# A state space layer put into a written order on four engines, with GpSimd two groups ahead and one behind, and a window attention with four score banks

## The chip, the cores and the metric

The kernel runs on one core of one Trainium2 chip. A core has five engines that run side by side, each with its own queue of instructions and ordered among each other by semaphores only: TensorE (PE, matrix products, with a separate row PEld for the loading of weights), VectorE (DVE), ScalarE (ACT), GpSimd (POOL) and SyncE (SP, which here issues every DMA). SBUF is the working memory, PSUM [...] takes the results of PE. The metric is the device time of the whole program in microseconds (us), as the median of several runs.

## The reference

Four images of 384 channels and 64 x 64 pixels go through two residual layers, all in float32. Each first normalizes its input over 32 groups of 12 channels (group norm).

```
x = x + state_space(gn(x))
x = x + window_attention(gn(x))

state_space, on L = 4096 tokens in row order:
  xn = layer norm over the 384 channels
  xb, z = split(xn @ in_proj)                     # 768 channels each
  xc = silu(causal conv of 4 taps over tokens (xb))
  dt, B, C = split(xc @ x_proj)                   # 24, 16 and 16 columns
  dt = softplus(dt @ dt_w + dt_b)
  for each token t, channel c, state n of 16:
      h[c,n] = exp(dt[t,c] * A[c,n]) * h[c,n] + dt[t,c] * xc[t,c] * B[t,n]
      y[t,c] = sum over n of h[c,n] * C[t,n]
  out = ((y + xc * D) * silu(z)) @ out_proj

window_attention: 12 heads of 32 channels; each pixel attends to the 7 x 7
  pixels around it (edge padded) with a relative bias; then a projection
```

## The kernel before, in words

The program takes one image after another: statistics of the input, `layer0` (state space), `layer1` (attention).

`layer0` holds channels in partitions (six blocks `d` of 128 channels) and tokens along the row, and works in 16 chunks of T = 256 tokens. In a chunk it runs over the six blocks and over four groups `g` of four states: 24 groups, each one call of `scan`. A group needs `db`, the product of dt, x and B for four states, 128 x 1024, which `driven` computes on GpSimd (L439, with `dtx` for a new block in L434). `scan` then works in two halves of two states: ScalarE computes da = exp(dt A) into one of the two PSUM banks of `ps_a` (L457), VectorE runs the recurrence along the tokens (L460), first into PSUM (`hp`), then into SBUF (`hs`); the last column is kept as the state for the next chunk (L466, L470). The product with C is VectorE's for `hp` (L467, into `hv`) and GpSimd's for `hs` (L471). PE transposes both against the identity and adds them up in `y` (L478). After four groups `turned` copies y on ScalarE (L488), turns it back on PE and adds xc D (L491, L496); `gated` multiplies with silu(z) (L504, VectorE). After six blocks `out_proj` runs (L516, L522).

Beside the scans of chunk i the preparation of chunk i+1 goes on. It is a Python generator (`prepared`, with `normed` called from it through `behind`), and `scan` takes one step of it with `next(ahead)` twice per group. `normed` is the group norm (L281, VectorE), the mean over channels by a product with ones (L287), subtraction, square, mean of squares, root by Ln and Exp, multiplication. `prepared` is the input projection (L310), the convolution as four products with diagonal matrices (L317), biases on ScalarE, six Silu in one block with a table load before and after, the product for dt, B and C (L331) with a trip of B and C through memory to spread them over partitions, and three softplus.

The order on the engines isn't that of the Python code: a planner orders each queue by its own estimates of costs. The order of the code only gives priorities, and the table-bound functions of ScalarE are kept in order by hand (`in_order`).

`layer1` works in eight stripes of eight rows, each with four blocks of 8 x 16 pixels, each with three steps `m` of four heads. A step is `scores` (four products of K = 32 rows into banks of `ps_l`, L727, a reduction on VectorE that adds the bias and finds the maximum, L733, an Exp on ScalarE), then for the step two back `attended` (L775), and for the one before `weighted`, the transposes of the weights (L752, L763) with their copies (L757, L767). At a block's end `block_end` turns the sums (L786 to L795), at a stripe's end `stripe_end` projects (L809, L814). Between, `projected` makes q, k and v of the next stripe (L632, L665, L695), one bank `mm` at a time; `window` loads the block of v that a block of pixels sees.

In the bank count of PSUM layer0 uses 2 + 1 + 2 + 3 = 8 (`ps_a`, `ps_h`, `ps_y`, `ps`), layer1 3 + 2 + 1 + 2 = 8 (`ps_l`, `ps_t`, `ps_v`, `ps`).

Of the kernel before, what the change touches and what calls it, by code (L numbers as in the profile page):

```python
# [8 lines left out]
F32 = mybir.dt.float32  # L9
AF = mybir.ActivationFunctionType  # L10
ALU = mybir.AluOpType
# [37 lines left out]
def two_layers(  # L49
# [22 lines left out]
    NB = x.shape[0]  # L72

# [180 lines left out]
    def layer0(b, x1, gm, st1):  # L254
        with ExitStack() as es:
            ps_a = es.enter_context(tc.tile_pool(name=f"ps_a{b}", bufs=2, space=PSUM))
# [6 lines left out]
            gm = gm(ps)  # L263

# [6 lines left out]
            def normed(i, h):  # L271
# [8 lines left out]
                for j in range(NJ):  # L280
                    nc.vector.tensor_scalar(  # L281
                        xn[:, j, :], src[:, j, :], gm[:, j, 0:1], gm[:, j, 1:2],
                        ALU.subtract, ALU.mult,
                    )
                mv = bank()
# [7 lines left out]
                )  # L293
                act(sq, xn, AF.Square)
                for j in range(NJ):
                    nc.tensor.matmul(
                        mv[:, 1, :], ones_c, sq[:, j, :], start=(j == 0), stop=(j == NJ - 1)
                    )
# [79 lines left out]
            def prepared(i, h):  # L378
# [31 lines left out]
                yield  # L410
                late = h["late"]()
                next(late, None)
                for t in h["xc"] + h["sz"]:
                    act(t, t, AF.Silu)
                load_exp_ln()
                yield
# [27 lines left out]
            def scan(d, g, h, db, y, ahead):  # L444
# [7 lines left out]
                hs = w2.tile([P, 2, T], F32, tag="hs", name="hs", bufs=3)  # L452
                for half, to in ((0, hp), (1, hs)):
# [11 lines left out]
                    if half == 0:  # L465
                        nc.vector.tensor_copy(state[:, d, n : n + 2], hp[:, :, T - 1])  # L466
                        nc.vector.tensor_tensor(hv, hp, ct[:, 0:2, :], ALU.mult)  # L467
                        next(ahead, None)
                    else:
                        nc.gpsimd.tensor_copy(state[:, d, n : n + 2], hs[:, :, T - 1])  # L470
                        nc.gpsimd.tensor_tensor(hs, hs, ct[:, 2:4, :], ALU.mult)  # L471

                for t in (hv, hs):
# [9 lines left out]
                next(ahead, None)  # L483
# [68 lines left out]
            db, late, ahead, y = driven(*work[0], steps[0]), None, iter(()), None  # L552
            done = iter(())
            for at, (i, d, g) in enumerate(work):
                if d == 0 and g == 0:
# [4 lines left out]
                    ahead = next_step()  # L560
                if g == 0:
                    y = ps_y.tile([P, 2, P], F32, tag="y", name="y")
                if (d, g) == (ND - 1, NS // NG - 1):
                    all_of(ahead)
                now = db
                if at + 1 < len(work):
                    nxt = work[at + 1]
                    db = driven(*nxt, steps[nxt[0]])
                scan(d, g, steps[i], now, y, ahead)
                next(done, None)  # L570
                if g == 3 and late is not None:
                    gated(*late)
                    if late[1] == ND - 1:
                        done = out_proj(late[0], late[2])
                if g == 1 and late is not None:
                    late = turned(*late)
                if g == NS // NG - 1:
                    late = (i, d, steps[i], y)
            late = turned(*late)
# [5 lines left out]
    def layer1(b, x1, gm):  # L585
        scale = HD**-0.5
        with ExitStack() as es:
            ps_l = es.enter_context(tc.tile_pool(name=f"ps_l{b}", bufs=3, space=PSUM))
            ps_t = es.enter_context(tc.tile_pool(name=f"ps_t{b}", bufs=2, space=PSUM))
            ps_v = es.enter_context(tc.tile_pool(name=f"ps_v{b}", bufs=1, space=PSUM))  # L590
            ps = es.enter_context(tc.tile_pool(name=f"ps1_{b}", bufs=2, space=PSUM))
# [209 lines left out]
            def stripe_end(s, aT):  # L801
                for m in range(NJ):
# [16 lines left out]
                    )  # L819

            pending, turned = None, None

            def attend():
# [4 lines left out]
                if m == NJ - 1:  # L828
                    block_end(bl, blk, aT)
                    if bl == NBLK - 1:  # L830
                        stripe_end(s, aT)
# [5 lines left out]
            for s in range(NXT):  # L837
# [5 lines left out]
                for bl in range(NBLK):  # L843
# [4 lines left out]
                    for m in range(NJ):  # L848
# [8 lines left out]
                        next(ahead, None)  # L857
# [7 lines left out]
            attend()  # L865

# [60 lines left out]
```

## Time and profile before

| | |
|---|---|
| time, median of 3 | 10455.0 us (10454.19 to 10461.72) |
| PE busy | 8126.5 us, 78% of the span |
| DVE busy | 7762.4 us, 74% |
| POOL busy | 6045.2 us, 58% |
| ACT busy | 5652.8 us, 54% |
| PEld busy | 5786.0 us, 55% |
| mean granted PE clock | 0.866 |
| scans of the first image | 178 to 1948 us |
| attention of the first image, first to last score | 2012 us to about 2670 us |

The share over the whole span averages two stages with different limits, so it is of little use by itself; the profile cuts the span in 40 slices and gives the busy tenths of each. A row of the groups reads: line, engine, operation, output from input with shapes and how often; then the busy time in all and the mean duration in nanoseconds of one; then the idle time of that engine just before these instructions and what ended it. A row of the waits reads: the engine and what it wanted to do, the work that released it, then the total in us, the number of times and the longest. A row of the timeline reads: start and length in us, engine, line, operation, shapes; in brackets the idle time before it.

### The profile page before, as it was taken

What the parts mean: (1) busy time and instruction counts of PE and PEld (TensorE: products, weight loads), DVE (VectorE), ACT (ScalarE), POOL (GpSimd) and SP (SyncE); (2) the same over time, 40 slices, a digit from 0 to 9 for tenths busy, and PEclk for the clock granted to TensorE, in tenths of its full rate; (3) what the DMA queues carried; (4) which work ended last, traced back from release to release, by engine and by line L of the source; (5) the groups of instructions that cost most, each with busy time, mean ns of one, the idle gap of its engine ahead of it and who ended that gap; (6) DMA issues with size and microseconds to landing.
All of it is one profiled execution on the core that took longest, in us unless ns stands there. A gap on an engine that the chain in (4) does not pass through costs nothing. (4 is left out here: it accounts for less than half of the span.)

```text
span 10459.5 us, 141089 instructions
## 1 busy us (share of the span) xinstructions
PE 8126.5 (78%) x46266; PEld 5786.0 (55%) x46266; DVE 7762.4 (74%) x15536; ACT 5652.8 (54%) x13502; POOL 6045.2 (58%) x5279
## 2 busy tenths in 40 slices
PE   4777777799777777779967777777996777777899
PEld 4565565455556556545556556554555556555455
DVE  4888888655588888855568888885556888888555
ACT  3666666344466666634446666653444666665344
POOL 3888888400388888830048888882005888888100
PEclk9888888799788888889978888888998888888899
DMA  2111111122111111112211111112212111111221
GB/s 79 55 42 41 53 42 40 59 75 65 67 46 42 51 43 42 50 58 79 58 68 42 43 51 42 45 46 69 70 56 69 39 55 42 41 53 38 71 71 54
DMA packets 300180, 563.69 MB, mean 54 GB/s; under 512 B 61197, under 2 KB 183325, under 8 KB 298805
## 3 DMA queue, kind: packets, MB, share of 16 engines
q1 hardware_dynamic: 299444, 554.67, 16.3%
q8 instruction: 366, 6.00, 0.2%
q14 instruction: 370, 3.02, 0.1%
HBM read 452.01 MB, written 84.73 MB: 51 GB/s over the span
## 5 line engine op out<-in xcount | busy, mean ns | idle before, releaser
L93 ACT ACTIVATE da<-dt,nega 128x256 f32<-128x256 f32 x6144 | 2902.2, 478 | 1563.9 <-DVE hs L460 851.0
L439 POOL TENSOR_TENSOR db<-dtx,B 128x1024 f32<-128x1024 f32 x1536 | 3619.7, 2357 | 0.0
L478 PE MATMUL y<-ident,hs 128*128 128x128 f32 x6144 | 1205.8, 329 | 1788.1 <-POOL hs L471 1785.9
L460 DVE TENSOR_TENSOR_SCAN hs<-da,state,db 128x256 f32<-128x256 f32 x3072 | 2217.6, 733 | 352.9 <-ACT da L93 333.9
L460 DVE TENSOR_TENSOR_SCAN hp<-da,state,db 128x256 f32<-128x256 f32 x3072 | 2290.1, 745 | 239.5 <-ACT da L93 101.5
L478 PEld LDWEIGHTS y<-ident,hs 128*128 128x128 f32 x6144 | 814.6, 165 | 2205.4 <-POOL hs L471 2180.5
L471 POOL TENSOR_TENSOR hs<-hs,C 128x512 f32<-128x512 f32 x1536 | 1949.5, 1269 | 5.4
L786 POOL COPY rb<-rsum 128x384 f32<-128x384 f32 x128 | 69.3, 541 | 2379.1 <-DVE rsum L784 2291.9
L310 PE MATMUL mm_ps<-xn,w_in 128*128 128x256 f32 x4608 | 1218.8, 404 | 7.7 <-DVE xn L303 7.7
L478 PE MATMUL y<-ident,hv 128*128 128x128 f32 x6144 | 1174.3, 325 | 46.4 <-DVE hv L467 46.0
L93 ACT ACTIVATE sg<-sg,mx 128x308 f32<-128x308 f32 x1536 | 830.9, 542 | 544.2 <-DVE mx L733 539.9
L478 PEld LDWEIGHTS y<-ident,hv 128*128 128x128 f32 x6144 | 926.2, 169 | 263.9 <-DVE hv L467 89.1
L467 DVE TENSOR_TENSOR hv<-hp,C 128x512 f32<-128x512 f32 x1536 | 1043.0, 679 | 0.0
L310 PEld LDWEIGHTS mm_ps<-xn,w_in 128*128 128x128 f32 x4608 | 898.6, 207 | 122.5 <-DVE xn L303 10.3
L470 POOL COPY state<-hs 128x2 f32<-128x2 f32 x1536 | 292.2, 190 | 1163.7 <-DVE hs L460 1048.5
L733 DVE CUSTOM_DVE_ANT_0 sg<-lg_ps,bias 128x308 f32<-128x308 f32 x1536 | 672.9, 475 | 322.2 <-PE lg_ps L727 269.6
L727 PE MATMUL lg_ps<-k,q 32*128 32x308 f32 x3072 | 695.2, 477 | 138.5 <-DVE mx L733 129.7
L317 PE MATMUL mm_ps<-xb,dcv 128*128 128x256 f32 x3072 | 748.9, 380 | 0.0
L767 ACT COPY tb<-pt_ps 88x512 f32<-88x512 f32 x384 | 223.2, 581 | 898.4 <-PE pt_ps L763 884.3
L757 DVE COPY ta<-pt_ps 110x512 f32<-110x512 f32 x768 | 494.0, 681 | 201.8 <-PE pt_ps L752 173.4
L317 PEld LDWEIGHTS mm_ps<-xb,dcv 128*128 128x128 f32 x3072 | 556.5, 191 | 63.3
L727 PEld LDWEIGHTS lg_ps<-k,q 32*128 32x128 f32 x3072 | 267.1, 185 | 521.9 <-DVE mx L733 290.1
(136 smaller groups left out, 11076.0 us busy)
## 6 DMA issues: line engine op xcount, KB each, us to landing
B<-bcrows SPq DMA_DIRECT2D x256, 512.0 KB
C<-bcrows SPq DMA_DIRECT2D x256, 512.0 KB
vw<-vd SPq DMA_DIRECT2D x1792, 33.0 KB
xr<-x SPq DMA_DIRECT2D x28, 1056.0 KB
vd<-v SPq DMA_DIRECT2D x280, 96.0 KB
xi<-in_x_dram SPq DMA_DIRECT2D x64, 384.0 KB
x<-in_x_dram SPq DMA_DIRECT2D x32, 768.0 KB
x<-xo SPq DMA_DIRECT2D x64, 384.0 KB
```

The costliest lines, as they stand in the source:

```text
L93: ins = nc.scalar.activation(o, i, func, **kw)
L310: nc.tensor.matmul(pb[:, k, :], w_in[:, j, m * P : (m + 1) * P], xn[:, j, :], start=(j == 0), stop=(j == NJ - 1),)
L317: nc.tensor.matmul(pb[:, k, :], dcv[:, d, c, :], xb[:, d, c : c + T], start=(c == 0), stop=(c == KC - 1),)
L439: nc.gpsimd.tensor_tensor(db, h["dtx"].unsqueeze(1).broadcast_to([P, NG, T]), h["bc"][g][0], ALU.mult)
L460: nc.vector.tensor_tensor_scan(to[:, k, :], da[:, k, :], db[:, 2 * half + k, :], state[:, d, n : n + 1], ALU.mult, ALU.add,)
L467: nc.vector.tensor_tensor(hv, hp, ct[:, 0:2, :], ALU.mult)
L470: nc.gpsimd.tensor_copy(state[:, d, n : n + 2], hs[:, :, T - 1])
L471: nc.gpsimd.tensor_tensor(hs, hs, ct[:, 2:4, :], ALU.mult)
L478: nc.tensor.matmul(y[:, half, :], t[:, k, half * P : (half + 1) * P], ident, is_transpose=True, start=(first and half == 0), stop=(last an ...
L727: nc.tensor.matmul(lg[:, :NK], blk["q"][pr, m, bl, :, :].rearrange("p r c -> p (r c)"), blk["k"][pr, m, :, bl * CB : bl * CB + CW], start= ...
L733: nc.vector.tensor_tensor_reduce(sg[:, hh, :], lg[:, :NK], bias[:, 4 * m + hh, :], -1.0, BIG, ALU.add, ALU.min, mx[:, hh : hh + 1],)
L757: nc.vector.tensor_copy(t[: KN[0], :, :].rearrange("p a q -> p (a q)"), pt[: KN[0], :])
```

## The change

In `layer0` the four compute engines leave the planner: inside `tc.manual_schedule(engines=in_step)` their queues have the order of the Python code (the DMA queue stays planned). The code is rewritten for that. GpSimd's `db` is made two groups ahead of the scans instead of one; its product of `hs` with C (now `with_c`) comes one group after the scans, and the sums on PE one group (`hv`) and two groups (`hs`) after. `hs` gets a fourth buffer. The group norm moves from VectorE to ScalarE, as scale and bias of an Identity, with `gb` = -mean x rstd. The chain of the layer norm gets more `yield`, so that each engine's part stands half a group after the one that feeds it. `turned` comes one group later and the gated product stays in the group after it.

In `layer1` the scores get four PSUM banks and the general pool `mm` one instead of two. So that the output projection needs only one bank at a time, `stripe_end` becomes a generator: one of its three parts in each of the following steps, in the place of a step of `projected`. The planner still orders this layer.

```
+    E = mybir.EngineType
+    in_step = {E.DVE, E.Activation, E.PE, E.Pool}
...
     def layer0(b, x1, gm, st1):
+            es.enter_context(tc.manual_schedule(engines=in_step))
...
+            gb = w1.tile([P, NJ, 1], F32, tag="gb", name=f"gb_{b}")
+            nc.vector.scalar_tensor_tensor(
+                gb, gm[:, :, 0:1], -1.0, gm[:, :, 1:2], ALU.mult, ALU.mult
+            )
...
                 for j in range(NJ):
-                    nc.vector.tensor_scalar(
-                        xn[:, j, :], src[:, j, :], gm[:, j, 0:1], gm[:, j, 1:2],
-                        ALU.subtract, ALU.mult,
-                    )
+                    act(
+                        xn[:, j, :], src[:, j, :], AF.Identity, scale=gm[:, j, 1:2],
+                        bias=gb[:, j, :],
+                    )
+                yield
...
+                yield
                 act(sq, xn, AF.Square)
+                yield
...
-                hs = w2.tile([P, 2, T], F32, tag="hs", name="hs", bufs=3)
+                hs = w2.tile([P, 2, T], F32, tag="hs", name="hs", bufs=4)
...
-                    else:
-                        nc.gpsimd.tensor_copy(state[:, d, n : n + 2], hs[:, :, T - 1])
-                        nc.gpsimd.tensor_tensor(hs, hs, ct[:, 2:4, :], ALU.mult)
-
-                for t in (hv, hs):
+                next(ahead, None)
+
+                def with_c():
+                    nc.gpsimd.tensor_copy(state[:, d, n : n + 2], hs[:, :, T - 1])
+                    nc.gpsimd.tensor_tensor(hs, hs, ct[:, 2:4, :], ALU.mult)
+
+                def summed(t):
...
+                return with_c, lambda: summed(hv), lambda: summed(hs)
...
+            AHEAD = 2
+            dbs = [driven(*w, steps[w[0]]) for w in work[:AHEAD]]
...
+                if at + AHEAD < len(work):
+                    if work[at + AHEAD][1:] == (0, 0):
+                        all_of(ahead)
...
+                if before:
+                    before[0][0]()
+                if at + AHEAD < len(work):
+                    nxt = work[at + AHEAD]
+                    dbs.append(driven(*nxt, steps[nxt[0]]))
+                if before:
+                    before[0][1]()
+                if len(before) > 1:
+                    before.pop()[2]()
                 next(done, None)
...
+                before.insert(0, scan(d, g, steps[i], dbs.pop(0), ys[d], ahead))
+                if g == 2 and late:
+                    late[0] = turned(*late[0])
+                if g == 3 and late:
+                    gated(*late[0])
...
     def layer1(b, x1, gm):
-            ps_l = es.enter_context(tc.tile_pool(name=f"ps_l{b}", bufs=3, space=PSUM))
+            ps_l = es.enter_context(tc.tile_pool(name=f"ps_l{b}", bufs=4, space=PSUM))
-            ps = es.enter_context(tc.tile_pool(name=f"ps1_{b}", bufs=2, space=PSUM))
+            ps = es.enter_context(tc.tile_pool(name=f"ps1_{b}", bufs=1, space=PSUM))
...
+                    yield True
...
-                        stripe_end(s, aT)
+                        ends.append(stripe_end(s, aT))
...
-                        next(ahead, None)
+                        if ends and next(ends[0], None) is None:
+                            ends.pop()
+                        elif not ends:
+                            next(ahead, None)
```

## The prediction

> **What bounds the kernel now.** I read the busy tenths first, because the program has two kinds of stages, four of each (one pair per image): the state space layer and the attention.
>
> ```profile
> PE   4777777799777777779967777777996777777899
> ...
> DVE  4888888655588888855568888885556888888555
> ...
> POOL 3888888400388888830048888882005888888100
> PEclk9888888799788888889978888888998888888899
> ```
>
> In the state space slices VectorE (DVE) and GpSimd (POOL) stand at 8 and TensorE (PE) at 7; in the attention slices PE stands at 9 and GpSimd at 0. First and last scan of each image lie 1769 us apart (178 to 1948 us in the first), so four layers take 7076 us; the rest is about 690 us of attention per image and the gaps around it.
>
> The groups of instructions by line name the work of the state space layer.
>
> ```profile
> L439 POOL TENSOR_TENSOR db<-dtx,B 128x1024 f32<-128x1024 f32 x1536 | 3619.7, 2357 | 0.0
> L460 DVE TENSOR_TENSOR_SCAN hs<-da,state,db 128x256 f32<-128x256 f32 x3072 | 2217.6, 733 | 352.9 <-ACT da L93 333.9 <-POOL db L439 5.5 <-PE y L478 5.4
> L471 POOL TENSOR_TENSOR hs<-hs,C 128x512 f32<-128x512 f32 x1536 | 1949.5, 1269 | 5.4
> L281 DVE TENSOR_SCALAR xn<-xi,gm_a 128x256 f32<-128x256 f32 x192 | 280.8, 1517 | 105.2 <-PE mm_ps L310 105.1
> ```
>
> 1536 is the number of "groups" (4 images x 16 chunks x 6 channel blocks x 4 state groups), so a group takes 1769/384 = 4.61 us and a chunk of 24 groups 110.6 us. The durations overlap at their ends, so I take pitches from the timeline, here GpSimd alone:
>
> ```profile
> 511.71 2.37 POOL L439 TENSOR_TENSOR db<-dtx,B 128x1024 f32<-128x1024 f32 x1
> 514.02 1.27 POOL L471 TENSOR_TENSOR hs<-hs,C 128x512 f32<-128x512 f32 x1
> 515.23 0.20 POOL L470 COPY state<-hs 128x2 f32<-128x2 f32 x1
> 515.37 2.37 POOL L439 TENSOR_TENSOR db<-dtx,B 128x1024 f32<-128x1024 f32 x1
> ```
>
> One group costs GpSimd 515.37 - 511.71 = 3.66 us, and every fourth one 0.73 us more (dtx, L434): 24 x 3.66 + 6 x 0.73 = 92.2 us per chunk. On VectorE the same timeline gives 3.39 us from scan to scan of undisturbed groups (511.15 to 514.54): 81.4 us, plus what it does once per chunk. So neither engine alone explains 110.6 us: they lose by waiting for each other. The waits say so.
>
> ```profile
> POOL state L470 <- DVE hs L460: 1048.5, 585, 7.5
> ACT da L93 <- DVE hs L460: 851.0, 803, 3.1
> DVE hs L460 <- ACT da L93: 333.9, 219, 2.8
> DVE yg L504 <- PE mm_ps L496: 293.7, 92, 4.8
> ```
>
> Taking the starts of the db products and their differences by place in the chunk shows where. The first 15 groups take 62.7 us (most are 3.66 or 4.4 us, one is 6.6 us at the wait for L496), the last nine 48.0 us, of which one group takes 10.1 us. That one is this, on VectorE:
>
> ```profile
> 460.78 5.28 DVE L281 TENSOR_SCALAR xn<-xi,gm_a 128x256 f32<-128x256 f32 x3
> 465.98 0.41 DVE L504 TENSOR_TENSOR yg<-mm_ps,sz 128x256 f32<-128x256 f32 x1
> 468.12 0.95 DVE L291 TENSOR_TENSOR xn<-xn,mm_ps 128x768 f32<-128x768 f32 x1 [1.74 <-PE mm_ps L287]
> ```
>
> **What the Trainium skill says.** "SBUF — State Buffer", section "SBUF: two separate sides": VectorE in a 2-port mode and GpSimd take one pair of ports under an exclusive lock, and the loser waits for the whole instruction. L281 agrees: 399 ns at best, 3820 ns at worst, mean 1517 ns, beside db products of 2357 ns. "TensorE: Matmul & The Clock Gate", Part 1: the PE clock is granted by activity. The trace agrees: 1.00 in attention, 0.71 in the sparse end of a chunk (697 to 734 us). Part 3 of the same page: matmuls on different 32-row strips of the array run side by side. It agrees too: six score passes take 0.80 us and two take 0.79 us. The specification table there calls the queues of the other engines strict first-in first-out, which matters for the written order.
>
> **The change part by part, state space layer.** Its four engines leave the planner and run in the order of the Python code.
>
> Group norm (L281) goes to ScalarE. VectorE loses 5.3 us per chunk; ScalarE gains 3 x 0.47 (an Identity of that shape, the xb row) = 1.4 us. ScalarE is about 61% busy (63 us of 100), so the sum fits, but where it stands matters: the three lie just ahead of the six Silu and two table loads, which in the trace run from 458.90 to 465.45 us with a 0.8 us piece of other work between, thus 5.8 us. No exponentials pass them. The timeline has 0.99 us for a pair of exponentials; ScalarE can be at most two pairs (the two da banks) ahead of the scans. From the end of one pair ScalarE needs 1.4 + 0.4 (ys copy) + 1.0 + 5.8 + 1.0 = 9.6 us to the second pair after it; VectorE has about 4.4 us of scans for that time. It stalls about 5.2 us per chunk. So of the 6.7 us that the 10.1 us group is too long, most stays: the L281 that went was lying beside this ScalarE block.
>
> The chain of the normalization (mean, subtract, square, mean, root, multiply) gets a yield between each engine, so the 1.74 us wait of L291 falls away.
>
> GpSimd: db two groups ahead of the scans, hs times C one group behind. No operation is added; the product no longer waits for the scan just ended, and the scans have two db in store. PE sums hv one group and hs two groups late, so the 1785.9 us that PE waits for hs should go; they cost little directly, but ScalarE's biases and the gated product (3.3 us, the 6.6 us group) queue behind PE. The gated product now comes a step after its transposes. New constraint: PE stands in line behind hs of two groups ago, and ScalarE's bias work behind PE; GpSimd may lag by perhaps half a group (2 us) and not by two.
>
> Sum for a chunk. First 15 groups: GpSimd 15 x 3.66 + 4 x 0.73 = 57.8 us; VectorE 15 x 3.39 + 3 gated x 0.4 + residual 1.1 + statistics 1.1 = 54.3. PE waits 13.2 of 63 us there, so needs 49.8. GpSimd bounds, less about 1.5 us of lag it may make up later: 56.3. Last nine: VectorE 30.5 + softplus 9 x 0.67 = 6.0 + L291 and L303 1.9 + gated 1.2 = 39.6, plus the 5.2 stall = 44.8; GpSimd 34.4; ScalarE 9 x 1.9 + softplus 10.8 + the rest some 10 = 38. Together 101.1 us against 110.6: 9.5 us x 64 chunks = 610 us. Bounds: perfect decoupling gives VectorE's 92.9 (24 x 3.39 + 11.5) plus part of the stall, 96.5 us (gain 900); if every ScalarE wait costs as before, 108 us (gain 170).
>
> **Attention.** It stays with the planner. With three score banks the fourth head waits for VectorE's first reduction:
>
> ```profile
> 10057.41 0.80 PE L727 MATMUL lg_ps<-k,q 32*128 32x308 f32 x6
> 10058.77 0.79 PE L727 MATMUL lg_ps<-k,q 32*128 32x308 f32 x2 [0.56 <-DVE mx L733]
> 10059.49 0.64 PE L775 MATMUL pv_ps<-ta,vw 110*32 110x128 f32 x16
> ```
>
> From the first score to pv is 2.08 us; one step earlier, where six passes were followed by pv at once, it is 0.73. Four banks give about 1.35 us less; VectorE's copies of ta then start later relative to PE, so I count 1.1. In the built order nine of a stripe's twelve steps have four scores in a row: 10 us of the 85.5 us of a stripe, seven stripes per image (the last has no projections), 70 us. Against it stands the single mm bank. In a stripe's end the built order puts three q projections nearly in a row, because the output projection, now spread over steps, has taken three or four steps of the next stripe's projections; each waits for a 0.75 us eviction: about 2 us. The last v rows reach memory later, two steps before their window is loaded, and that window's fourteen transfers take 6 us to issue: 0 to 4 us, I take 1.5. In all 3.5 x 7 = 25. The first projection of an image (42 us, fifteen banks in a row) can't overlap eviction with matmuls any more: some 5 us more beyond what the half clock hides. Net 70 - 25 - 5 = 40 us per image, 160 us in all; between 0 and 300.
>
> Forecast: 10455 - 610 - 160 = 9685 us.
>
> **Rivals.** (A) The forecast, 9685. (B) Both engines run near their own sums: 96.5 us a chunk and the full attention gain, 10455 - 900 - 300 = 9255. For it: the 3.66 us runs are exact, so nothing but waits stands between. Against it: the Silu block and five groups of softplus, where ScalarE is nearly full. (C) The written order only moves the waits: PE's cold clock at the start of a chunk delays the biases, these delay exponentials in a strict queue, 108 us a chunk, and the single bank eats the attention's gain: 10455 - 170 - 50 = 10235. For it: the 0.71 clock, and that each group already needs all four engines. (D) Convoys: each queue blocked by its oldest wait, a group at 5.1 us, or 122.4 us a chunk: 64 x 11.8 = 755 us lost, 160 gained: 11050. For it: a planner filled gaps that no order of mine can see. Against it: in the built order every cross-engine pair stands at least half a group apart.
>
> **How the numbers follow.** A 0.60, B 0.15, C 0.18, D 0.07. The likeliest gives 9685. A with its own spread and C make up 0.78; the range from 9320 (between A and B) to 10100 (most of C) leaves out about 0.2. Faster by over 0.2%: A, B and C but for a little, 0.92; within 0.2%: 0.01; slower: 0.07.
>
> **What would show it.** Right: db products 4.2 us apart on average; L281's successor on ScalarE at about 0.47 us each; the waits of PE for hs nearly gone; GpSimd at 9 tenths in the state space slices; one gap of about 5 us per chunk left at the Silu block; score passes in eights with pv 0.8 us after. Wrong: VectorE waiting for da at every group (ScalarE in line behind PE), GpSimd waiting for hs scans as before, PE waiting for q's eviction or for the window at each stripe's end, or a stripe still at 85 us.

## The result, and the profile after

The changed kernel takes 10500.5 us (median, 10500.0 to 10504.6) against 10457.9 us before: a ratio of 1.0042, 95% interval [1.0024, 1.0059]. It is slightly slower, where 9685 us had been forecast. Line numbers from here on are those of the changed kernel (db L453, scans L474, hv L481, state copy and product on GpSimd L486 and L487, sums L495, softplus' products L370 and corrections L384 to L386, all of ScalarE's functions L96).

First the busy tenths of the changed kernel, to be laid beside those of before.

```profile
PE   4677777699777777769967777777996777777799
...
DVE  3888888655588888865568888886556888888655
...
POOL 3788878500388878850048878884004877888300
PEclk9788878799878877879988877887998877887899
```

VectorE still stands at 8 and GpSimd at 7 to 8, not at 9, and the clock granted to TensorE is a tenth lower in many of these slices (mean 0.847, before 0.866). In the first image the first and last scan lie 1821 us apart (185.5 to 2006.9 us) instead of 1769, so four state space layers lost some 208 us; the program as a whole lost 43, so the rest gained about 165.

The page's groups confirm that GpSimd's two products did not become dearer (mean ns behind the bar, 2357 and 1269 before); the scans stay at 0.73 to 0.75 us:

```profile
L453 POOL TENSOR_TENSOR db<-dtx,B 128x1024 f32<-128x1024 f32 x1536 | 3613.2, 2353 | 30.1
...
L487 POOL TENSOR_TENSOR hs<-hs,C 128x512 f32<-128x512 f32 x1536 | 1944.8, 1266 | 123.2 <-POOL state L486 0.8
```

The successor of L281 on ScalarE takes 100.5 us in all. What changed is who waits for whom (total us, times, longest):

```profile
POOL state L486 <- DVE hs L474: 1146.8, 529, 6.9
PE y L495 <- DVE hv L481: 973.3, 634, 3.5
...
ACT spe L96 <- PE mm_ps L370: 575.8, 118, 5.8
...
DVE hs L474 <- ACT da L96: 425.0, 177, 4.4
...
DVE hp L474 <- ACT da L96: 313.1, 120, 4.7
PE y L495 <- POOL hs L487: 190.3, 209, 3.0
```

The wait of TensorE for GpSimd's product fell from 1785.9 to 190.3 us, as meant. In its place stands a wait for VectorE's product (46.0 us before), ScalarE's wait for softplus' products rose from 146.7 to 575.8 us, and VectorE's waits for the exponentials rose together from 435 to 738 us. GpSimd waits for the scans as it did (1048.5 before).

By place in the chunk, from the differences of the db starts, the first 15 groups take 63.7 us (56.3 forecast), the last nine 52.4 (44.8 forecast); the chunk is 116.1 us. The same count gives 62.4, 49.1 and 111.5 us for the kernel before: the prediction's 110.6 is the mean of all sixteen chunks of an image, and that takes in the last one, beside which no preparation runs. On that reckoning the changed kernel has 113.8 us (1821/16).

That last chunk is worth a look. From its first to its last scan it takes 91.4 us in the changed kernel and 101.4 before. Where no preparation runs, the written order gains 10 us a chunk; it loses 4.6 in the chunks that also hold the preparation of the next one.

Seven neighbouring groups of such a chunk take 44.8 us, with single ones of 7.3 and 10.4. They hold the Silu block and the three softplus of the next chunk. This is the timeline of one of them:

```profile
3230.81 0.69 DVE L386 TENSOR_TENSOR dt<-dt,mm_ps 128x512 f32<-128x512 f32 x1
...
3231.55 2.07 PE L370 MATMUL mm_ps<-xd,w_dt 24*128 24x256 f32 x4 [3.42 <-DVE dt L386]
...
3233.66 0.47 ACT L96 ACTIVATE spe<-mm_ps,dtb 128x256 f32<-128x256 f32 x1 [5.78 <-PE mm_ps L370]
...
3235.10 1.01 ACT L96 ACTIVATE da<-dt,nega 128x256 f32<-128x256 f32 x2
...
3236.20 1.55 DVE L474 TENSOR_TENSOR_SCAN hp<-da,state,db 128x256 f32<-128x256 f32 x2 [4.37 <-ACT da L96]
```

VectorE's correction of one softplus (L386) holds up TensorE's product for the next, ScalarE's Abs waits for it, the exponentials stand behind Abs in ScalarE's queue, and VectorE waits for the exponentials. One chain through three engines, and it closes on itself, since the corrections of the next softplus stand behind those scans in VectorE's queue.

Waiting is not all of it. This table splits a chunk with preparation, as VectorE sees it, into work and waits of more than 0.15 us (from the traces, mean of the second to the 13th chunk of each image; the kernels between are those of the experiments; the forecast's waiting is what its 101.1 us leave beside the 92.9):

| VectorE, us a chunk | chunk | at work | waiting |
|---|---|---|---|
| before | 111.5 | 98.4 | 13.1 |
| the change | 116.1 | 97.6 | 18.5 |
| pe_free | 114.8 | 97.7 | 17.2 |
| pe_act_free | 110.2 | 97.5 | 12.7 |
| planned | 105.8 | 93.5 | 12.4 |
| only_pool | 102.1 | 92.9 | 9.1 |
| the forecast's sum | 101.1 | 92.9 | 8.2 |

VectorE lost 4.4 us of group norm a chunk (280.8/64) and is only 0.8 less at work. The comparison of the engines' orders below shows where the rest went.

### The profile page after: what moved, and what is told of

The parts are those of the page before. It is cut to its first block, busy times and chain, and to the rows that moved or that the text cites. A ratio compares the mean times of both kernels' runs of the same rounds, so it can differ in the third digit from the quotient of the medians.

```text
span 10502.9 us, 139329 instructions
## 1 busy us (share of the span) xinstructions
PE 7956.0 (76%) x46266; PEld 5775.4 (55%) x46266; DVE 7691.6 (73%) x15348; ACT 5804.4 (55%) x13694; POOL 6107.8 (58%) x5279
## 5 line engine op out<-in xcount | busy, mean ns | idle before, releaser
L96 ACT ACTIVATE da<-dt,nega 128x256 f32<-128x256 f32 x6144 | 2920.8, 477 | 1373.3 <-DVE hs L474 863.6
L453 POOL TENSOR_TENSOR db<-dtx,B 128x1024 f32<-128x1024 f32 x1536 | 3613.2, 2353 | 30.1
L474 DVE TENSOR_TENSOR_SCAN hp<-da,state,db 128x256 f32<-128x256 f32 x3072 | 2305.7, 751 | 714.6 <-ACT da L96 313.1
L474 DVE TENSOR_TENSOR_SCAN hs<-da,state,db 128x256 f32<-128x256 f32 x3072 | 2125.4, 734 | 425.2 <-ACT da L96 425.0
L487 POOL TENSOR_TENSOR hs<-hs,C 128x512 f32<-128x512 f32 x1536 | 1944.8, 1266 | 123.2 <-POOL state L486 0.8
L495 PE MATMUL y<-ident,hv 128*128 128x128 f32 x6144 | 1244.8, 338 | 973.7 <-DVE hv L481 973.3
L495 PEld LDWEIGHTS y<-ident,hv 128*128 128x128 f32 x6144 | 904.2, 173 | 1423.7 <-DVE hv L481 1049.1
L495 PE MATMUL y<-ident,hs 128*128 128x128 f32 x6144 | 1198.1, 330 | 193.5 <-POOL hs L487 190.3
L96 ACT ACTIVATE sg<-sg,mx 128x308 f32<-128x308 f32 x1536 | 830.2, 542 | 883.1 <-DVE mx L765 881.9
L321 PE MATMUL mm_ps<-xn,w_in 128*128 128x256 f32 x4608 | 1178.3, 400 | 41.3 <-DVE xn L314 41.3
L495 PEld LDWEIGHTS y<-ident,hs 128*128 128x128 f32 x6144 | 923.4, 173 | 277.1 <-POOL hs L487 277.0
L481 DVE TENSOR_TENSOR hv<-hp,C 128x512 f32<-128x512 f32 x1536 | 1048.9, 683 | 0.0
L486 POOL COPY state<-hs 128x2 f32<-128x2 f32 x1536 | 285.2, 186 | 1157.0 <-DVE hs L474 1146.8
L509 PE MATMUL mm_ps<-ident,ys 128*128 128x128 f32 x768 | 200.5, 351 | 676.4 <-ACT ys L506 676.4
L328 PE MATMUL mm_ps<-xb,dcv 128*128 128x256 f32 x3072 | 703.6, 379 | 0.0
L448 POOL TENSOR_TENSOR dtx<-dt,xc 128x256 f32<-128x256 f32 x384 | 279.5, 728 | 466.4 <-DMA C<-bcrows 297.2
L534 PE MATMUL mm_ps<-yg,w_out 128*128 128x256 f32 x2304 | 532.0, 381 | 0.0
L509 PEld LDWEIGHTS mm_ps<-ident,ys 128*128 128x128 f32 x768 | 101.5, 165 | 779.7 <-ACT ys L506 767.7
```

The costliest lines, as they stand in the source:

```text
L96: ins = nc.scalar.activation(o, i, func, **kw)
L321: nc.tensor.matmul(pb[:, k, :], w_in[:, j, m * P : (m + 1) * P], xn[:, j, :], start=(j == 0), stop=(j == NJ - 1),)
L328: nc.tensor.matmul(pb[:, k, :], dcv[:, d, c, :], xb[:, d, c : c + T], start=(c == 0), stop=(c == KC - 1),)
L453: nc.gpsimd.tensor_tensor(db, h["dtx"].unsqueeze(1).broadcast_to([P, NG, T]), h["bc"][g][0], ALU.mult)
L474: nc.vector.tensor_tensor_scan(to[:, k, :], da[:, k, :], db[:, 2 * half + k, :], state[:, d, n : n + 1], ALU.mult, ALU.add,)
L495: nc.tensor.matmul(y[:, half, :], t[:, k, half * P : (half + 1) * P], ident, is_transpose=True, start=(first and half == 0), stop=(last an ...
```

## The experiments

All times are medians, with the ratio to the kernel before measured beside them and its 95% interval.

**Which layer loses?** Two kernels each take one layer from the old program and one from the new.

> The kernel before with the new attention alone (four score banks, one bank for the rest, the stripe's end spread over steps); the state-space layer is the old, planned one. Theory (the written order of the state-space layer loses what the attention gains): the image period of before and after differ by 10.4 us while the state-space stretch grew by 52, so the attention gains about 41 us an image, 4 x 41 = 165: 10,290 us (10,250 to 10,330). Rival (the single bank eats the gain and the state-space layer is even): 10,440 to 10,480.

> The new state-space layer with the old attention. Theory: 10,458 + 4 x 52 = 10,665 us (10,620 to 10,710). Rival (the state-space layer is even, the loss is the attention's): 10,440 to 10,480.

New attention alone: 10288.9 us, 0.984 [0.9825, 0.9854]. New state space layer alone: 10673.5 us, 1.0206 [1.0191, 1.0221]. The attention gains 172 us; the state space layer loses about 212, as the traces had said. In the attention a stripe fell from 85.5 to 79.5 us, and the way from the last scan to the first score grew by 5 us.

**Which wait is it?** My first theory was that TensorE, standing at the sum of hv, delays the products for the biases and so everything behind. Two edits attack it from both ends: the sum one group later, and the pieces of preparation (`next(ahead)`) behind both pairs of exponentials.

```
-                if before:
-                    before[0][1]()          # hv_late (hv gets a third buffer)
                 if len(before) > 1:
+                    before[1][1]()
                     before.pop()[2]()
...
```
```
                         nc.vector.tensor_tensor(hv, hp, ct[:, 0:2, :], ALU.mult)
-                        next(ahead, None)   # exps_first
+                next(ahead, None)
                 next(ahead, None)
```

> The kernel after, but TensorE's sum of a group's first half (hv) is put one group later in the written order, beside the sum of its second half, with a third hv buffer (and one chunk buffer of x fewer, to make room). Theory (TensorE stands at hv, the products for ScalarE's biases lie behind it, the exponentials behind these, VectorE waits for them): the 973 us wait of the hv sum goes to under 200, ScalarE's waits for TensorE's products (576, 428 and 316 us) fall by half or more, and the chunk goes from 116 to 104 to 110 us: 9,750 to 10,150. Rival 1 (GpSimd's pitch of 3.79 sets the time, TensorE's wait is idle time that nobody feels): 10,450 to 10,500, the waits moved to the second half's product. Rival 2 (ring of three banks sets it): 10,400 to 10,500.

> The kernel after, but both pieces of the next chunk's preparation come behind the group's second pair of exponentials instead of one between the two pairs. Theory (exponentials stand in line behind biases that wait for TensorE): VectorE's wait for the exponentials (425 and 313 us) falls by half, the chunk by 3 to 6 us: 10,100 to 10,300. Rival (TensorE's product is late in any case, the first pair of the next group then waits as long): 10,450 to 10,550.

hv_late: 10454.7 us, 0.9996 [0.9987, 1.0004], only 46 us better than the changed kernel. The wait for hv is nearly gone (39 us against 206 in the stretch from 2950 to 4500 us), but a wait of 146 us for the product of hs stands in its place, and the groups of 7.3 and 10.4 us stay (6.4 and 10.4). So the theory falls in this form: TensorE's place in line at hv is not what costs. That it stands in line at all isn't tested by this, since it now stands at hs; pe_free below frees its order as a whole. exps_first: 10398.2 us, 0.9943 [0.9926, 0.9959], 102 us better: exponentials that stand behind biases are a part of it, and not the whole.

**Is it the ring of PSUM banks, or the longer norm?** A bank is here one PSUM buffer of up to 128 x 512 values, and the pool `ps` of `layer0` has three, used in turn. L370 waits for L386 because one of three banks is with the norm's means, one with the turned sums and one with the softplus before. bank_early lets softplus keep 1+e in SBUF; norm_short takes away three of the norm's new steps, so that its bank comes free early; bank_first is bank_early with exps_first. (hv_late, bank_early, bank_first and the two kernels spread below also have one buffer of the input x fewer, to make room; in none of their traces does a compute engine wait for that transfer.)

```
-                act(pb, e, AF.Identity, bias=1.0)      # bank_early
+                act(u, e, AF.Identity, bias=1.0)       # u in SBUF, also in Ln and L384 to L386
```

> The kernel after, but softplus keeps 1+e in SBUF instead of writing it back into its PSUM bank, so the bank is free after Abs and Relu and not only after VectorE's last correction (and one chunk buffer of x fewer, to make room). Theory (the third softplus of a chunk has no bank: of the ring of three the norm's means hold one, the turned sums one, the second softplus one, so TensorE's L370 waits for L386, ScalarE for L370 and the exponentials behind it for both, 5.8 + 4.4 us once a chunk): the 191.7 us wait of L370 for L386 disappears, the 10.4 us group falls to 5 to 6, 64 x 4 to 5 us: 10,180 to 10,250. Rival (the exponentials stand behind TensorE's product anyway, bank or no bank): 10,450 to 10,500.

> The kernel after, but three of the norm's steps that it had given a step of their own (subtraction, square, sum of squares) are taken in one, as in the kernel before, so the norm's bank is free before the softplus starts. Theory of the ring of banks: the wait of L370 for L386 disappears and the second softplus no longer stands behind the sum of squares; the price is a longer stall at the Silu block, where the square waits for VectorE: net 3 to 8 us a chunk, 9,990 to 10,310. Rival (ring of banks without weight): 10,450 to 10,550.

> The kernel after with two edits at once: softplus' bank freed early and the pieces of preparation behind both pairs of exponentials. If the two are separate stalls the gains add: 10,398 less 250 to 320, so 10,080 to 10,150. If the exponentials' order alone had already taken the wait out of the way: 10,350 to 10,400.

bank_early: 10499.7 us, 1.0049 [1.0034, 1.0064], no gain. The wait of L370 did disappear and the group of 10.4 us became one of 6.3, but the two beside it grew from 7.3 to 8.3 and 8.9: seven groups, 44.1 us. A part of that is a new cost, seen in the durations of the corrections (minimum, median, maximum in ns), which now read only SBUF:

```profile
L386 DVE TENSOR_TENSOR spu<-spr,spu x41: 691/692/2719, 2984.1 to 4494.4; 128x512 f32<-128x512 f32 x41
```

In the changed kernel, with one operand in PSUM, the same instruction (there L385) takes 0.70 us on average. The Trainium skill, "SBUF — State Buffer", section "SBUF: two separate sides", has it that a VectorE instruction with two SBUF inputs takes the ports that it shares with GpSimd while a GpSimd instruction reads SBUF too, and that the later of the two waits for the whole of the earlier. The trace agrees: of the 192 instructions of L386, 64 took 2.71 to 2.72 us, each of these began while a db product ran (2.67 us beside the longest), and none of the other 128 did. Together the three corrections grew from 2.07 to 3.6 us in the mean, 4.6 us a chunk, about what the bank had given. So the ring of banks was not cleanly tested here. norm_short tests it at another price, which its expectation names: 10543.4 us, 1.0088 [1.0073, 1.0103]; the wait is gone, the Silu block's group grows to 9.5, and seven groups are 44.8 us again. bank_first: 10340.0 us, 0.9898 [0.9881, 0.9914], 58 us below exps_first and outside both of its expectations, close to the one that had the exponentials' order take the wait out of the way. What the ring costs by itself stays open.

**GpSimd's turn.** The db starts lie 3.79 us apart in the even stretches, and lay 3.66 apart before. Back to back, copy and product start 0.27 us apart; with db between them the copy cost 0.14. pool_split restores the old sequence: state copy, db, product.

> The kernel after, but GpSimd's order in a group is state copy, next db, product with C, as the planner had it, instead of copy, product, db. If GpSimd's turn of 3.79 us instead of 3.66 is what counts in the even stretches: 0.13 us in about 15 places, 64 x 2 us: 10,350 to 10,400. Rival: the product with C comes 2.3 us later and TensorE's sum of the second half, the pieces behind it and ScalarE wait for it: 10,550 to 10,750.

10700.8 us, 1.0239 [1.0224, 1.0254]. The turn is 3.65 again (3003.50 to 3007.15 us on its timeline), and the kernel is 200 us slower. The rival was right in size: the product comes later and TensorE waits for it (608.8 us against 190.3). That sum alone isn't the 200 us, as TensorE's wait for hv fell at the same time from 973.3 to 674.9. Its way through the engines is read from one stretch: after such a wait (3324.72 us) the product for the biases starts late, ScalarE waits 4.46 us for it, and exponentials and scans stand behind.

**Is the stretch too crowded for ScalarE?** spread keeps all instructions and changes the pace: a bias shares its step with the next product, and each softplus is cut into five steps.

```
                     with_bias(xb[:, d : d + 2, KC - 1 :], pb, binp[:, d : d + 2])
-                    yield            # the same after the other two biases
...
                     act(r[:, k, :], pb[:, k, :], AF.Relu, bias=bias)
-                yield
+                    yield
                 act(e, e, AF.Exp, scale=-1.0)
+                yield
```

> The kernel after with the same instructions in another pace: the biases no longer take a half-group step of their own (18 steps instead of 27 before the Silu block), and each softplus is cut into five steps instead of three (buffers: six for the gate, three for x). New theory (the seven groups that hold the Silu block, the norm and three softplus take 44.8 us instead of 28 because ScalarE has some 35 us of work in them, in line with the exponentials, while the seventeen others run at GpSimd's 3.79): the excess of 16.7 us falls by a third to two thirds, 5 to 11 us a chunk: 9,800 to 10,180. Rival (every piece that stands between exponentials costs the same wherever it stands, as hv_late, bank_early and norm_short suggest, whose totals are the same within 1 us a chunk): 10,430 to 10,530.

> The pace of the run 'spread', with the pieces behind both pairs of exponentials as in 'exps_first'. New theory: the two gains add in part: 9,750 to 10,100, below the kernel with the new attention alone (10,289). Rival: 10,350 to 10,450, as exps_first alone.

Spread: 10667.5 us, 1.0204 [1.0188, 1.0219]; with exponentials first 10639.2, 1.0177 [1.0162, 1.0193]. Both theories miss: it is 167 us worse. The pace did become more even in places, but the Silu block came to stand just ahead of the copy of y (`ys`), for which TensorE waits; the w_xp product stands behind that, and ScalarE's copy `xd` behind w_xp. A group of 12.9 us arose there. This is VectorE and ScalarE in it:

```profile
3112.04 0.99 ACT L96 ACTIVATE da<-dt,nega 128x256 f32<-128x256 f32 x2
...
3113.12 1.55 DVE L472 TENSOR_TENSOR_SCAN hp<-da,state,db 128x256 f32<-128x256 f32 x2 [4.72 <-POOL db L451]
...
3118.97 0.37 ACT L347 COPY xd<-mm_ps 56x256 f32<-56x256 f32 x1 [5.94 <-PE mm_ps L342]
```

The first wait is labelled with db, but the scan starts 1.08 us after its exponentials (3112.04 us), as others do, and these came right after the Silu block: the block is the cause. The second is ScalarE standing at xd with the exponentials behind it, for which VectorE then waits another 3.93 us.

**The written order itself, and the group norm.** planned is the changed kernel without `manual_schedule`; gn_dve has the group norm as in the old code, in the written order.

```
-            es.enter_context(tc.manual_schedule(engines=in_step))
```

> The kernel after without the written order: the planner orders all engines from the same code (GpSimd two ahead and one behind only as far as its priorities keep it, group norm on ScalarE, the same buffers). Theory (the written order is what loses): 10,100 to 10,300, with VectorE 5 us a chunk lighter at best 9,950. Rival (the new pieces themselves lose, not their order): 10,450 to 10,650.

> The kernel after with the group norm back on VectorE (tensor_scalar, as before), in the written order. If ScalarE's load in the crowded stretch is what limits: no slower, 10,400 to 10,520. If VectorE's own time counts there as well: plus up to 64 x 5.3 us, 10,600 to 10,840. The prediction gave this edit 3.6 to 5.3 us a chunk.

Planned: 9980.5 us, 0.9545 [0.9531, 0.956], which is 520 us less than the changed kernel, from the same operations. gn_dve: 10554.1, 1.0098 [1.0081, 1.0115]: in the written order the group norm on ScalarE is worth 54 us, 0.8 us a chunk. The planned kernel's waits show what did not matter:

```profile
PE y L494 <- POOL hs L486: 921.7, 644, 3.6
...
POOL state L485 <- DVE hs L473: 773.5, 539, 7.1
```

TensorE waits nearly five times as long for hs as in the changed kernel. GpSimd waits for the scans a third less, and VectorE for the exponentials of the second half 207.3 us instead of 425.0.

**Which engine's order?** Four more kernels change only the set of engines that are held to the written order (`in_step`): all but TensorE (pe_free), all but ScalarE (act_free), VectorE and GpSimd only (pe_act_free), GpSimd only (only_pool). planned_gn is planned with the group norm on VectorE, planned_first is planned with the pieces behind both pairs.

> The kernel after with TensorE's order left to the planner; ScalarE, VectorE and GpSimd keep the written order. If the loss is a loop of TensorE's and ScalarE's strict queues, freeing one of them gives back more than half of the 520 us: 10,000 to 10,250. If ScalarE's written order alone does it (exponentials behind biases, Silu and softplus): 10,400 to 10,500.

> The kernel after with ScalarE's order left to the planner; TensorE, VectorE and GpSimd keep the written order. Loop of two queues: 10,000 to 10,250. TensorE's order alone: 10,400 to 10,500.

> The kernel after with TensorE and ScalarE left to the planner; VectorE and GpSimd keep the written order, GpSimd strictly two ahead and one behind. If the loop of TensorE and ScalarE is the whole loss: 9,950 to 10,050, as the planned kernel (9,980), or below it. If VectorE's and GpSimd's written order have a part: 10,100 to 10,400.

> The planned kernel (no written order) with the group norm back on VectorE. If the edit is worth what the prediction took from VectorE's 5.3 us a chunk: 9,980 + 64 x 3.6 to 5.3, so 10,210 to 10,320. If ScalarE's added work eats it, as in the written order (where it was worth 0.9 us a chunk): 9,980 to 10,060.

> The kernel after with only GpSimd in the written order; TensorE, ScalarE and VectorE are planned. If GpSimd's strict order holds the 195 us (a turn of 3.79 us instead of 3.66 in some fifteen groups of a chunk is 64 x 2 = 125 us by itself): 10,100 to 10,180. If VectorE's written order holds them: 9,970 to 10,030.

> The planned kernel with the pieces of preparation behind both pairs of exponentials in the program's order. If the order in the program carries over to the planner: 9,880 to 9,960. If the planner had already placed them so: 9,960 to 10,000.

| held to the written order | us | ratio to before |
|---|---|---|
| none (planned) | 9980.5 | 0.9545 [0.9531, 0.956] |
| GpSimd (only_pool) | 9717.3 | 0.9298 [0.9283, 0.9314] |
| GpSimd, VectorE (pe_act_free) | 10175.4 | 0.9727 [0.9712, 0.9741] |
| GpSimd, VectorE, TensorE (act_free) | 10188.1 | 0.9739 [0.9724, 0.9753] |
| GpSimd, VectorE, ScalarE (pe_free) | 10441.7 | 0.9984 [0.9977, 0.9991] |
| all four (the change) | 10500.5 | 1.0042 [1.0024, 1.0059] |

planned_gn 9976.7, 0.9534 [0.9519, 0.9548]; planned_first 9973.2, 0.9542 [0.9528, 0.9556]: neither can be told from planned. Of the expectations, those on one loop of TensorE and ScalarE fall: TensorE's order costs 13 us with ScalarE planned (0.1%; the single runs, 10,183 to 10,196 against 10,173 to 10,182 us, just don't overlap) and 59 with it held, ScalarE's 266 and 312. And my guess on the remaining 195 us, from planned to pe_act_free, was wrong on both sides: VectorE's order costs 458 us, while GpSimd's alone gains 263. only_pool is the fastest kernel of all, 783 us below the changed one.

Why VectorE's order costs is seen between pe_act_free and only_pool at the same work. There are two parts. The first is VectorE's own turn. This is an undisturbed group in the written order (pe_act_free):

```profile
2950.60 1.53 DVE L474 TENSOR_TENSOR_SCAN hp<-da,state,db 128x256 f32<-128x256 f32 x2
2952.16 0.16 DVE L480 COPY state<-hp 128x2 f32<-128x2 f32 x1
2952.24 0.68 DVE L481 TENSOR_TENSOR hv<-hp,C 128x512 f32<-128x512 f32 x1
2952.84 1.38 DVE L474 TENSOR_TENSOR_SCAN hs<-da,state,db 128x256 f32<-128x256 f32 x2
2954.14 1.52 DVE L474 TENSOR_TENSOR_SCAN hp<-da,state,db 128x256 f32<-128x256 f32 x2
```

and in the planner's order (only_pool):

```profile
3005.47 1.53 DVE L474 TENSOR_TENSOR_SCAN hp<-da,state,db 128x256 f32<-128x256 f32 x2
3006.91 0.72 DVE L474 TENSOR_TENSOR_SCAN hs<-da,state,db 128x256 f32<-128x256 f32 x1
3007.55 0.13 DVE L480 COPY state<-hp 128x2 f32<-128x2 f32 x1
3007.60 0.68 DVE L481 TENSOR_TENSOR hv<-hp,C 128x512 f32<-128x512 f32 x1
3008.20 0.74 DVE L474 TENSOR_TENSOR_SCAN hs<-da,state,db 128x256 f32<-128x256 f32 x1
3008.86 1.52 DVE L474 TENSOR_TENSOR_SCAN hp<-da,state,db 128x256 f32<-128x256 f32 x2
```

The instructions are the same and take equally long, but the turn is 3.54 us in the first and 3.39 in the second. The copy of the state reads the scan right ahead of it and starts when that has ended; the planner puts a scan between that doesn't need it, and that starts before the one ahead has ended. The median of undisturbed groups is 3.55 to 3.56 us in every kernel that holds VectorE to the written order, and 3.38 to 3.41 in every one that doesn't. Over the scans of the first image the views by window give the stretch, its length and VectorE's busy time, pe_act_free first:

```profile
177.95:1919.70 1741.75, 1515.37 (x2635) 0.83 0.13 43
181.60:1808.10 1626.50, 1459.37 (x2639) 0.83 0.14 46
```

56 of the 115 us between them are longer busy time at the same work. No run changed only the place of that copy, so the size of this part is read from the traces and not from an experiment.

The second part is waiting. In pe_act_free, behind a group's hv product:

```profile
3120.50 0.69 DVE L384 SCALAR_TENSOR_TENSOR mm_ps<-mm_ps,spe 128x512 f32<-128x512 f32 x1
...
3121.22 0.69 DVE L385 TENSOR_TENSOR mm_ps<-spr,mm_ps 128x512 f32<-128x512 f32 x1
...
3121.95 0.69 DVE L386 TENSOR_TENSOR dt<-dt,mm_ps 128x512 f32<-128x512 f32 x1
...
3122.55 0.95 DVE L314 TENSOR_TENSOR xn<-xn,mm_ps 128x768 f32<-128x768 f32 x1
...
3123.42 1.38 DVE L474 TENSOR_TENSOR_SCAN hs<-da,state,db 128x256 f32<-128x256 f32 x2
...
3124.84 0.99 ACT L96 ACTIVATE da<-dt,nega 128x256 f32<-128x256 f32 x2 [4.03 <-DVE hs L474]
...
3124.87 0.19 POOL L486 COPY state<-hs 128x2 f32<-128x2 f32 x1 [2.78 <-DVE hs L474]
```

VectorE is busy all the time, but 2.9 us of corrections and norm stand in one block ahead of the hs scans (and each correction waits for the end of the one before: 0.72 us from L384 to L385). Meanwhile ScalarE has no bank for the next exponentials (4.03 us) and GpSimd no result (2.78 us). In only_pool the planner puts single scans between the same corrections, and the next instruction follows L385 after 0.61 us:

```profile
3071.80 0.69 DVE L385 TENSOR_TENSOR mm_ps<-spr,mm_ps 128x512 f32<-128x512 f32 x1
3072.41 0.75 DVE L474 TENSOR_TENSOR_SCAN hp<-da,state,db 128x256 f32<-128x256 f32 x1
3073.07 0.67 DVE L386 TENSOR_TENSOR dt<-dt,mm_ps 128x512 f32<-128x512 f32 x1
3073.66 0.74 DVE L474 TENSOR_TENSOR_SCAN hp<-da,state,db 128x256 f32<-128x256 f32 x1
```

and on ScalarE single exponentials between the parts of softplus:

```profile
3067.35 0.65 ACT L96 ACTIVATE spe<-spe 128x512 f32<-128x512 f32 x1
...
3067.87 0.49 ACT L96 ACTIVATE da<-dt,nega 128x256 f32<-128x256 f32 x1
...
3068.27 0.61 ACT L96 ACTIVATE mm_ps<-spe 128x512 f32<-128x512 f32 x1
```

Its waits, to be held against the 1146.8, 425.0 and 313.1 us of the changed kernel:

```profile
POOL state L486 <- DVE hs L474: 348.4, 361, 7.3
...
DVE hp L474 <- ACT da L96: 235.5, 144, 2.6
...
DVE hs L474 <- ACT da L96: 187.0, 64, 4.7
```

GpSimd's wait for the scans falls with the time in these five kernels: 1147 us in the changed kernel, 1048 before, 786 in pe_act_free, 774 in planned, 348 in only_pool. It is no measure for all of them: bank_first has 751 us at 10340 us. The Trainium skill, "Perfetto Trace Analysis", section "Optimizing Scalar/DVE Operations", says that where VectorE and ScalarE are not full but cause gaps elsewhere, smaller pieces may let work end sooner; no run here shows that, since the instructions stay as they are and only the blocks of them are broken up. That the blocks are the cause of this second part is read from such stretches too; no run moved them alone.

One rival was not tested by itself: the granted clock of TensorE is lower in the changed kernel (0.847) than before (0.866) and highest in only_pool (0.877). TensorE's busy time is not longer for it, 7956.0 us against 8126.5, so it may be an effect of the waits.

## Why the prediction was wrong

Step by step:

- **What bounds the kernel: right.** Two engines that lose by waiting for each other. only_pool has half of the changed kernel's waiting and takes 9717 us, 32 us from the forecast; its chunk is 102.1 us (forecast 101.1). Part of that closeness is luck: its first 15 groups take 60.9 us (forecast 56.3) and its last nine 41.2 (forecast 44.8), and the two errors offset each other.
- **L281 to ScalarE: credited with too much.** VectorE did lose the 280.8 us of L281. With all engines planned that was worth nothing (9976.7 with it, 9980.5 without): there VectorE waits for the norm's means instead, 315.8 us against 19.5. In the written order it was worth 54 us. Each instruction on ScalarE takes 0.59 us, not 0.47. The stall at the Silu block stays, as said: 3.80 us of waiting in the trace, where I had 5.2.
- **The wait of TensorE for hs: right in size, wrong in weight.** It went as foreseen. But planned and only_pool keep 922 and 559 us of it and take the least time.
- **The failing steps.** The sum has 92.9 us of VectorE's own work and 8.2 us of waiting in a chunk; measured are 97.6 and 18.5 us.
  The first step that failed is "24 x 3.39": the turn of VectorE was taken from the planned kernel and carried over to an order of the code in which an instruction stands right behind the one that it needs. There the turn is 3.55 us, 3.8 us a chunk more, nearly all that the loss of L281 (4.4 us) had given.
  The second is "New constraint: PE stands in line behind hs of two groups ago, and ScalarE's bias work behind PE; GpSimd may lag by perhaps half a group (2 us) and not by two." I named one line of waiting and put it at nothing, and even took 1.5 us off for lag to be made up. In the runs several queues stand still at once: exponentials behind biases and softplus on ScalarE (its order costs 266 to 312 us over the program), scans behind the corrections on VectorE (a part of the 458 us of its order, the rest being its longer turn), and least of all the line I named, TensorE's (13 to 59 us). These are differences along one chain of additions and need not add up in another.
- **The sum for the last nine groups** took VectorE's 39.6 us of work plus one stall, and let ScalarE's 38 us and GpSimd's 34.4 run beside it. In the written order they run partly after each other: 52.4 us. With the planner on all but GpSimd they do run beside each other: 41.2 us, below the 44.8 forecast.
- **The sum for the first 15 groups**, 57.8 less 1.5, was mis-sized for GpSimd: its turn in the new sequence is 3.79 us, not 3.66, which makes 59.8, and the lag was not made up. only_pool takes 60.9, the changed kernel 63.7.
- **Attention: right.** 160 us forecast, 172 measured. The parts fit as well: 6 us a stripe (10 less 3.5 forecast) and 5 us lost in an image's first projection (5 forecast).
- **The rivals.** C had the mechanism (exponentials in a strict queue behind biases behind a slow TensorE) but priced it at 108 us a chunk; D priced convoys at 122.4. The 113.8 us (the mean of all chunks, as they counted) lie between. The argument against D, that each pair of engines stands half a group apart, is the one that did not hold: half a group is 1.9 us, while VectorE's corrections of one softplus take 2.1 us in a row and ScalarE's Silu block some 6.

What stays open: which part of the new code gives planned its 308 us over the kernel with the new attention alone (the group norm is none of it; the fourth hs buffer, the order of the calls and the extra steps were not taken apart), what VectorE's order costs without GpSimd's, and what the written order would take with an independent scan between the hp scans and the copy of their state, or with the corrections spread among the scans.

## What to carry to other kernels

A fixed order is worth holding on the engine whose work is uniform and which should run ahead: here GpSimd alone, 263 us. On VectorE and ScalarE, which mix a steady chain (scans, exponentials) with blocks of other work, it cost more than it gave, in part because each block stands ahead of the chain and other queues stop with it; moving one wait or one piece mostly moved the stall, as four edits here showed (hv_late, bank_early, norm_short, spread). The other part is cheap to look for: a turn that was measured in one order of the instructions does not hold in another. If you write the order yourself, put an independent instruction between two that depend on each other, and measure the turn again. Before pricing an order by each engine's own sum, it seems worth while (no run here tests it) to take the longest block that it puts ahead of the chain and to compare it with the slack of the buffers behind it.

## What the runs showed of the hardware

- A VectorE instruction that reads two SBUF operands of 128x512 (L386 of bank_early) takes 0.69 us, and up to 2.72 us when it starts while GpSimd's db product runs; with one operand in PSUM (L385 of the changed kernel) it takes 0.70 us at most.
- A VectorE instruction that reads the result of the one right ahead starts later than one that doesn't. From L384 to L385, which needs it, it is 0.72 us (3120.50 to 3121.22 us in pe_act_free); from L385, equally long, to a scan that doesn't need it 0.61 us (3071.80 to 3072.41 us in only_pool).
- GpSimd shows something alike: its small state copy costs 0.14 us when another product follows it and 0.27 us when the product on the same tile follows.
- TensorE's four w_dt passes take 1.13 us in two of the three softplus of a chunk and 2.07 us in the third, before which TensorE had waited 3.42 us.
